# A one-core twelve-layer linear-attention kernel: the last bias's token shares move from the prologue to behind layer 2, and the first masking is left to VectorE

## The chip, the core and the metric

The kernel runs on one core of one Trainium2 chip. The metric is the device time of one execution in microseconds (us). The five engines are called by their short names: PE is TensorE (PEld is its weight load), DVE is VectorE, ACT is ScalarE, POOL is GpSimd, SP is SyncE, which here only issues transfers.

## The reference, cut to what matters

The input is x with 16 sequences of 256 tokens and 128 features. Twelve attention layers without a softmax follow each other, each with 16 heads of 8 features. After them come a layer norm, one gated feed-forward block with 384 hidden features, and a second layer norm.

```python
for i in range(12):
    qkv = x @ Wqkv[i].T + bqkv[i]
    q, k, v = split(qkv)                    # 16 heads of 8
    att = einsum('bhqd,bhkd->bhqk', q, k) / sqrt(8)
    y = einsum('bhqk,bhkd->bhqd', att, v)
    x = y @ Wproj[i].T + bproj[i] + x
x = layernorm(x0 + x)
x = layernorm(x + (silu(x @ wg.T) * (x @ wu.T)) @ wd.T)
```

Because nothing nonlinear stands between q, k and v, a layer acts on a sequence's tokens as one affine map. Everything about the tokens that a layer needs is their Gram matrix and their mean.

## The kernel before, in words

**What is tiled.** The 16 sequences form 8 pairs (`p`), and the pairs form two halves (`o`), four pairs each. For each sequence the kernel keeps a 128 x 128 matrix T and one more column, the token mean's image c; both lie in the tile `tst` (130 columns for a sequence, 260 for a pair). A layer updates T and c; the tokens themselves are only touched at the end, when T is applied to them and the feed-forward part runs.

**The prologue** (`prologue`) makes from each pair's tokens the Gram matrix (PE, L336), the means (DVE, L340 to L342), and the centred Gram matrix `g0` (tile `g`, DVE, L353, two instructions for a pair). L353 needs the mean laid out as a row, which PE transposes (L346) and ACT or DVE copies into `kv` (L205 or L207).

**One layer** has these steps. `products` multiplies T by the key and value weights (PE L434 to L436, from the second layer on), by the query weights (L442 to L444), and `g0` by the value side (L455; in the first layer straight from the raw weights `wraw`), and copies each result out of its accumulator bank. `heads` multiplies keys with that per group of 32 rows (L499), adds the offsets on DVE (L509, tile `gm`), keeps only the head blocks (the masking of `gm`, a multiplication by `mask32`, L213 by helper), and multiplies with the queries in 32 x 32 tiles (L517, "y" below). `projection` splits y into a high and a low part (`yhl`: the high part by ACT or DVE at L205 or L207, the low part by DVE at L530), multiplies by the projection weights (PE L534 to L536), adds to T on DVE (L541), and splits the new T (`thl`: high part on ACT at L205, low part on POOL at L210).

**Weights** are split the same way into `whl`: a copy by ACT or DVE (L205 or L207) and a subtraction by POOL (L210). SP then issues transfers that turn the projection weights (`wpt`, L305, L306). In the first layer's stage the weights of the layers 1 and 2 are split.

**The step that is moved.** `shares` has two DVE steps and one product: it adds the last layer's projection bias to the token means (L410), multiplies by the centring matrix on PE (L411, 128 x 16), and copies the result back to the tile `mb` (L412). Only the last layer reads `mb`.

**What sets the order.** Each engine runs its instructions strictly in the order in which the program holds them. That order is made when the kernel is built, by a list scheduler (`Plan.run`). Every step carries estimated costs for the engines that may do it, what it reads and writes, and a priority number, mostly the layer's number with small offsets. The scheduler repeatedly takes, among the steps that can start first, the one with the lowest priority number (with a tiny weight for the length of what depends on it), puts it on the engine where it is estimated to end first, and gives it one of eight accumulator banks. So a step that is given another place or other engines also moves other steps, and copies between ACT and DVE, elsewhere.

The first masking was free to go to either engine, and `shares` stood after the prologue with a priority near layer 8, although the scheduler takes a later priority early where nothing else can start:

```python
plan.op({DVE: dve(OB * 32), POOL: pool(OB * 32)}, lambda e: mul(e, gm, gm, mask32...), [], [vgm[o]], prio)
...
shares(L - 4)
```

Of the kernel before, what the change touches and what calls it, by code (L numbers as in the profile page):

```python
# [14 lines left out]
ALU = mybir.AluOpType  # L15
# [3 lines left out]
L = 12  # L19
# [19 lines left out]
OB = G * PB  # L39
# [34 lines left out]
PE, ACT, DVE, POOL, SP = "pe", "act", "dve", "pool", "sp"  # L74
# [100 lines left out]
def act(n, sbuf=False, pointers=0):  # L175
    return (94 if sbuf else 51) + 93 * pointers + n / 1.2


def dve(n, fast=False):
    return 69 + n / (1.92 if fast else 0.96)  # L180


def pool(n):
    return 147 + 2.1 * n
# [7 lines left out]
def linear_attention_ffn_kernel(ctx: ExitStack, tc: tile.TileContext, x, xt, wall, wq0, bias, wg, wu, wd, out):  # L192
    nc = tc.nc
# [5 lines left out]
    plan = Plan({"bank": 8, "raw": RAW, "weights": WSLOTS, "turned": WSLOTS})  # L199
# [12 lines left out]
    def mul(e, dst, a, b):  # L212
        (nc.vector if e == DVE else nc.gpsimd).tensor_tensor(dst, a, b, ALU.mult)  # L213
# [26 lines left out]
    bcol, wq0s = new("bcol", [L, 4]), new("wq0s", [C])  # L240
# [12 lines left out]
    mask32 = new("mask32", [32])  # L253
# [7 lines left out]
    vbias, vwq0 = Val(), Val()  # L261
# [53 lines left out]
    means = new("means", [B])  # L315
# [6 lines left out]
    vt, vc, vhi, vlo, vm, vg0, vkv, vyh, vyl, vqo, vw = (named() for _ in range(11))  # L322
# [34 lines left out]
    def center_tokens(p, prio):  # L357

        bs = slice(p * PB, (p + 1) * PB)
        x3 = xts[p].rearrange("p (b t) -> p b t", t=T)  # L360
        vn = Val()
        plan.op({POOL: 150}, lambda e: nc.gpsimd.tensor_scalar(nmeans[:, bs], means[:, bs], -1.0, 0.0, ALU.mult, ALU.add), [vm[p]], [vn], prio)
        for b in range(PB):
            plan.op({ACT: act(T, True, 1)}, lambda e, b=b: nc.scalar.activation(
                x3[:, b, :], x3[:, b, :], AF.Identity, bias=nmeans[:, p * PB + b : p * PB + b + 1]), [vn], [vx[p]], prio)
# [5 lines left out]
    def offset_products(l, o):  # L371

        raw, pc = wts[l][0], Val("bank")
        c = tst[:, o * OB : (o + 1) * OB, C]

        def mm():
            for s in range(1 if l else 0, 3):
                for g in range(G):
                    cols = slice(32 * g, 32 * g + 32)
                    nc.tensor.matmul(bank(pc)[cols, s * OB : (s + 1) * OB], wraw[raw.slot][:, s * C : (s + 1) * C][:, cols], c, start=True, stop=True)  # L380
        return [raw, *vc[o * G : (o + 1) * G]], pc, mm

    def offsets(l, o, prio, pc):


        bs, ps = slice(o * OB, (o + 1) * OB), slice(o * G, (o + 1) * G)
        c = tst[:, bs, C]
        step = lambda costs, f, reads, writes: plan.op(costs, f, reads, writes, prio)
        src = lambda s: bank(pc)[:, s * OB : (s + 1) * OB]
        step({DVE: 133}, lambda e: nc.vector.tensor_scalar(vb[:, bs], src(2), bcol[:, l, 2:3], None, ALU.add), [pc, vbias], [vvc[o]])  # L390
        step({DVE: 133}, lambda e: nc.vector.tensor_scalar(kb[:, bs], src(1), bcol[:, l, 1:2], float(T), ALU.add, ALU.mult), [pc, vbias], [vkb[o]])
        if l == 0:
            step({DVE: 133}, lambda e: nc.vector.tensor_scalar(qc[:, bs], src(0), bcol[:, 0, 0:1], None, ALU.add), [pc, vbias], [vqc[o]])
        step({DVE: dve(32 * OB)}, lambda e: nc.vector.transpose(flat(vbb[:, bs]), vb[:, bs].unsqueeze(2).to_broadcast([128, OB, 32])), [vvc[o]], [vvb[o]])
        step({DVE: dve(32 * OB)}, lambda e: mul(e, kvo[:, bs], vbb[:, bs], kb[:, bs].unsqueeze(2).to_broadcast([128, OB, 32])), [vvb[o], vkb[o]], [vkvo[o]])

        if l < L - 1:
            def share(e):
                if e == ACT:
                    nc.scalar.activation(c, c, AF.Identity, bias=bcol[:, l, 3:4])  # L400
                else:
                    nc.gpsimd.tensor_scalar(c, c, bcol[:, l, 3:4], 0.0, ALU.add, ALU.add)
            step({POOL: 200, ACT: 220}, share, [vbias, *(vhi[ps] if l else [])], vc[ps])

    mb, vmb = new("mb", [B]), Val()

    def shares(prio):

        pc = Val("bank")
        plan.op({DVE: 133}, lambda e: nc.vector.tensor_scalar(mb, means, bcol[:, L - 1, 3:4], None, ALU.add), [vbias, *vm], [vmb], prio)  # L410
        plan.op({PE: 214}, lambda e: nc.tensor.matmul(bank(pc)[:, :B], center, mb, start=True, stop=True), [vmb], [pc], prio)  # L411
        plan.op({DVE: 133}, lambda e: nc.vector.tensor_copy(mb, bank(pc)[:, :B]), [pc], [vmb], prio)  # L412

# [2 lines left out]
    vgm = sets()  # L416
# [55 lines left out]
    def first_offsets(o, prio):  # L472
        def fill(e):
            for p in range(o * G, (o + 1) * G):
                nc.gpsimd.tensor_copy(qss[p][:, :, C], qc[:, p * PB : (p + 1) * PB])
        plan.op({POOL: 600}, fill, [vqc[o]], vqo[o * G : (o + 1) * G], prio)

    def heads(l, o, prio, riders):

        raw = wts[l][0]
        pairs = range(o * G, (o + 1) * G)
        gm = gms[o]
        pm, pys = Val("bank"), [Val("bank") for _ in pairs]
        group = lambda g: slice(32 * (g % G), 32 * (g % G) + 32)
        src = [raw] if l == 0 else [vkv[p] for p in pairs]

        more = [(*r, *offset_products(*r)) for r in riders]

        def mm_m(e):
            for _, _, _, _, mm in more:
                mm()
            for p in pairs:
                for b in range(PB):
                    n = (p - o * G) * PB + b
                    tk = wraw[raw.slot][:, C : 2 * C] if l == 0 else kvs[p][:, b, 0, :]
                    for g in range(G):
                        nc.tensor.matmul(bank(pm)[group(g), n * 32 : n * 32 + 32], tk[:, group(g)], gvs[p][:, b, group(g)], start=True, stop=True)  # L499
        reads = [v for _, _, rs, _, _ in more for v in rs]  # L500
        if l == 0 and o == 1:

            reads += vw[:G]
        plan.op({PE: 890 + 140 * len(more)}, mm_m, [*(vgv[p] for p in pairs), *src, *reads], [pm, *(m[3] for m in more)], prio)
        for lo, oo, _, pc, _ in more:
            offsets(lo, oo, prio + (OFFSET if lo else 0), pc)
            if lo == 0:
                first_offsets(o, prio)
        plan.op({DVE: dve(OB * 32)}, lambda e: nc.vector.tensor_tensor(  # L509
            gm, bank(pm)[:, : OB * 32].rearrange("p (b j) -> p b j", j=32), kvo[:, o * OB : (o + 1) * OB], ALU.add), [pm, vkvo[o]], [vgm[o]], prio)  # L510
        plan.op({DVE: dve(OB * 32), POOL: pool(OB * 32)}, lambda e: mul(e, gm, gm, mask32.unsqueeze(1).to_broadcast([128, OB, 32])), [], [vgm[o]], prio)

        def mm_y(e):
            for b in range(PB):
                for r, p in enumerate(pairs):
                    for g in range(G):
                        nc.tensor.matmul(bank(pys[r])[group(g + r), b * W : (b + 1) * W], gm[group(g), r * PB + b, :], qss[p][group(g), b, :], start=True, stop=True)  # L517
        plan.op({PE: 1200}, mm_y, [vgm[o], *(vq[p] for p in pairs), *(vqo[p] for p in pairs)], pys, prio)
        return pys
# [68 lines left out]
    def prep_ffn(prio):  # L588
        for n, src in (("g", wg), ("u", wu), ("d", wd)):
            raw = Val("raw")  # L590
            ints = lambda raw=raw: wraw[raw.slot][:, : NH * C].bitcast(I32)
            plan.op({SP: 192 * 5}, lambda e, src=src, ints=ints: nc.sync.dma_start(ints(), src), [], [raw], prio)
            plan.op({ACT: act(384, True), DVE: dve(384, True)}, lambda e, n=n, ints=ints: copy(e, fw[n], ints()), [raw], [vfw[n]], prio)
# [152 lines left out]
    prep_weights(0)  # L746
    for p in range(NP):
        prologue(p, -1 if p < G else LATE)
    shares(L - 4)
    for o in range(NO):  # L750
        first_q(o, -0.5 if o == 0 else 0.03)
    for l in range(L):
        if l + 1 < L:
            prep_weights(l + 1)
        for o in range(NO):
            at = l + OSTEP * o
            for p in range(o * G, (o + 1) * G):
                products(l, p, at)
            for r, py in enumerate(heads(l, o, at, [(l, o)] * (l < OWN) + [(l + o, 1 - o)] * (OWN <= l + o < L))):
                projection(l, o * G + r, py, at + (LSTEP * r if l == L - 1 else 0))  # L760
        if l < NP:
            center_tokens(l, l + 2)
    prep_ffn(L - 2)
    picks(L - 4)
    for p in range(NP):
# [35 lines left out]
```

## Time and profile before

| what | value |
| --- | --- |
| three runs, median (lowest to highest) | 305.5 us (305.44 to 306.06) |
| the profiled execution's own time | 305.16 us |
| its span, first to last instruction | 303.2 us |
| around the span | 1.96 us |
| busy: PE, PEld, DVE, ACT, POOL | 294.3, 269.8, 226.1, 217.7, 137.8 us |
| granted PE clock over the span | 0.998 |

The profiled execution is 0.34 us shorter than the median of the three runs. A timeline row gives the start, the time from the first start to the last end of the group, the engine, the line, the operation, what is written and read, and how many instructions the row merges. On PE a 32-bit product shows as two instructions for each weight load in the program, so "x4" of L455 is one pair's two products.

### The profile page before, as it was taken

The numbers are of one execution on the slowest core, as the hardware profiler recorded it, in microseconds if no ns is written. First come the engines' busy times: TensorE is split into PE (matmuls) and PEld (weight loads), VectorE is DVE, ScalarE is ACT, GpSimd is POOL, SyncE is SP. The second block draws the span as 40 slices with busy tenths as digits, with TensorE's granted clock in tenths as the row PEclk, the third lists the DMA queues.
The fourth block names the chain that finished last, engine by engine and source line by source line (L and its number), as shares of the span: only waits on it lengthen the run. The fifth ranks groups of instructions, "written<-read, shape, count | busy, mean of one in ns | idle before, by whom it ended". The sixth has DMA issues, their size and how long they took to land.

```text
span 303.2 us, 12834 instructions
## 1 busy us (share of the span) xinstructions
PE 294.3 (97%) x5376; PEld 269.8 (89%) x5376; DVE 226.1 (75%) x683; ACT 217.7 (72%) x559; POOL 137.8 (45%) x208
## 2 busy tenths in 40 slices
PE   8999999999999999999999999999999999999981
PEld 8989999999999999999999999989999998878760
DVE  4796887777677676876767777786644789999993
ACT  3556877867777768777686666777887558788875
POOL 8256452334531445225432354224431167777883
PEclk9999999999999999999999999999999999999999
DMA  7624213112031120311302102120000000000225
GB/s 214 163 91 131 67 39 89 38 46 82 3 89 37 39 89 4 88 40 28 98 2 56 37 17 50 49 68 17 2 2 4 3 1 2 0 0 8 63 70 138
DMA packets 22489, 15.65 MB, mean 52 GB/s; under 512 B 1952, under 2 KB 19872, under 8 KB 22432
## 3 DMA queue, kind: packets, MB, share of 16 engines
q1 hardware_dynamic: 21872, 14.62, 17.3%
q8 instruction: 42, 0.69, 0.9%
q10 hardware_dynamic: 560, 0.22, 0.3%
q14 instruction: 15, 0.12, 0.1%
HBM read 8.02 MB, written 2.10 MB: 33 GB/s over the span
## 4 chain that ended last, share of the span: by engine, by line
PE 87%; DVE 10%; issue 1%; ACT 1%; POOLq 0%; POOL 0%; DVEq 0%
PE bank L455 14%; PE bank L434 8%; PE bank L517 8%; PE bank L436 7%; PE bank L435 7%; PE bank L442 5%; PE bank L499 5%; PE bank L536 4%; PE bank L534 4%; PE bank L535 4%; PE bank L443 3%; PE bank L444 3%; PE bank L336 3%; DVE st L618 2%; PE bank L706 2%; PE bank L707 2%
## 5 line engine op out<-in xcount | busy, mean ns | idle before, releaser
L210 POOL TENSOR_TENSOR thl<-tst,thl 128x260 fp32r<-128x260 f32 x88 | 64.8, 768 | 123.1 <-ACT thl L205 123.1
L205 ACT COPY qgv<-bank 128x256 f32<-128x256 f32 x169 | 59.8, 378 | 19.2 <-PE bank L444 12.9
L205 ACT COPY kv<-bank 128x512 f32<-128x512 f32 (+1 forms) x93 | 53.4, 575 | 19.5 <-PE bank L436 14.2
L434 PE MATMUL bank<-whl,thl 128*128 128x256 f32 x176 | 51.9, 295 | 0.0
L436 PE MATMUL bank<-whl,thl 128*128 128x256 f32 x176 | 49.7, 282 | 0.0
L435 PE MATMUL bank<-whl,thl 128*128 128x256 f32 x176 | 49.4, 281 | 0.0
L455 PE MATMUL bank<-kv,g 128*128 128x128 f32 x352 | 46.1, 275 | 0.0
L541 DVE TENSOR_TENSOR tst<-bank,tst 128x260 f32<-128x260 f32 x96 | 36.9, 425 | 9.4 <-PE bank L536 9.0
L205 ACT CAST thl<-tst 128x260 fp32r<-128x260 f32 x88 | 33.0, 408 | 14.6 <-DVE tst L541 14.5
L455 PEld LDWEIGHTS bank<-kv,g 128*128 128x128 f32 x352 | 42.7, 191 | 0.4 <-issue 0.4
L448 DVE TENSOR_SCALAR qgv<-bank,bcol 128x2 f32<-128x2 f32 x88 | 19.2, 221 | 28.3 <-ACT qgv L205 22.9
L434 PEld LDWEIGHTS bank<-whl,thl 128*128 128x128 f32 x176 | 33.1, 188 | 4.0 <-issue 3.8
L530 DVE TENSOR_TENSOR yhl<-bank,yhl 128x260 fp32r<-128x260 f32 x96 | 34.4, 420 | 2.2 <-ACT yhl L205 2.1
L436 PEld LDWEIGHTS bank<-whl,thl 128*128 128x128 f32 x176 | 33.1, 188 | 0.3 <-POOL thl L210 0.2
L435 PEld LDWEIGHTS bank<-whl,thl 128*128 128x128 f32 x176 | 33.2, 189 | 0.0
L442 PE MATMUL bank<-thl,whl 128*128 128x260 f32 x88 | 28.8, 327 | 0.0
L205 ACT CAST yhl<-bank 128x260 fp32r<-128x260 f32 (+1 forms) x61 | 21.8, 408 | 8.3 <-PE bank L517 7.7
L207 DVE CAST yhl<-bank 128x260 fp32r<-128x260 f32 (+1 forms) x43 | 16.7, 430 | 12.7 <-PE bank L517 12.7
L517 PE MATMUL bank<-qgv,gm 32*32 32x130 f32 x1536 | 25.8, 280 | 0.2 <-DVE gm L213 0.2
L443 PE MATMUL bank<-thl,whl 128*128 128x260 f32 x88 | 24.8, 282 | 0.0
L444 PE MATMUL bank<-thl,whl 128*128 128x260 f32 x88 | 24.7, 281 | 0.0
L517 PEld LDWEIGHTS bank<-qgv,gm 32*32 32x32 f32 x1536 | 17.2, 103 | 5.5 <-ACT kv L205 0.3
(157 smaller groups left out, 694.7 us busy)
## 6 DMA issues: line engine op xcount, KB each, us to landing
wraw<-wall SPq DMA_DIRECT2D x12, 256.0 KB, 3.0
wpt<-whl SPq DMA_DIRECT2D x24, 96.0 KB, 2.2
qgv<-x SPq DMA_DIRECT2D x8, 256.0 KB, 5.0
xt<-xt SPq DMA_DIRECT2D x8, 256.0 KB, 3.1
out<-kv SPq DMA_DIRECT2D x7, 256.0 KB, 2.3
wpt<-whl SPq DMA_DIRECT2D x24, 64.0 KB, 2.7
wpt<-whl SPq DMA_DIRECT2D x24, 32.0 KB, 1.9
wraw<-wg SPq DMA_DIRECT2D x1, 192.0 KB, 3.2
```

The costliest lines, as they stand in the source:

```text
L205: nc.scalar.copy(dst, src)
L210: (nc.vector if e == DVE else nc.gpsimd).tensor_tensor(dst, a, b, ALU.subtract)
L434: nc.tensor.matmul(o, hi[:, b, 0:C], hl(0, 1, 2), start=True, stop=False)
L435: nc.tensor.matmul(o, hi[:, b, 0:C], hl(1, 1, 2), start=False, stop=False)
L436: nc.tensor.matmul(o, lo[:, b, 0:C], hl(0, 1, 2), start=False, stop=True)
L442: nc.tensor.matmul(o, hl(0, 0), flat(hi), start=True, stop=False)
L443: nc.tensor.matmul(o, hl(0, 0), flat(lo), start=False, stop=False)
L444: nc.tensor.matmul(o, hl(1, 0), flat(hi), start=False, stop=True)
L455: nc.tensor.matmul(bank(pgv)[:, b * C : (b + 1) * C], g0[p][:, b, :], tv(b), start=True, stop=True)
L517: nc.tensor.matmul(bank(pys[r])[group(g + r), b * W : (b + 1) * W], gm[group(g), r * PB + b, :], qss[p][group(g), b, :], start=True, stop= ...
L530: plan.op({DVE: dve(PB * W)}, lambda e: nc.vector.tensor_tensor(yl, bank(py)[:, : PB * W], yh.bitcast(F32), ALU.subtract), [py, vyh[p]], [ ...
L541: plan.op({DVE: dve(PB * W)}, lambda e: nc.vector.tensor_tensor(ts, bank(pw)[:, : PB * W], ts, ALU.add), [pw], [vt[p], vc[p]], prio)
```

## The change

Two edits. `shares` is called within the loop over layers, after layer 2, with a priority of 4, and its first DVE step now also waits for the T of all pairs (`vt`). The masking of the first half in the first layer may only be done by DVE; every other masking can still go to either engine.

```diff
-    def shares(prio):
+    def shares(prio, behind):
 
         pc = Val("bank")
-        plan.op({DVE: 133}, lambda e: nc.vector.tensor_scalar(mb, means, bcol[:, L - 1, 3:4], None, ALU.add), [vbias, *vm], [vmb], prio)
+        plan.op({DVE: 133}, lambda e: nc.vector.tensor_scalar(mb, means, bcol[:, L - 1, 3:4], None, ALU.add), [vbias, *vm, *behind], [vmb], prio)
         plan.op({PE: 214}, lambda e: nc.tensor.matmul(bank(pc)[:, :B], center, mb, start=True, stop=True), [vmb], [pc], prio)
         plan.op({DVE: 133}, lambda e: nc.vector.tensor_copy(mb, bank(pc)[:, :B]), [pc], [vmb], prio)
...
-        plan.op({DVE: dve(OB * 32), POOL: pool(OB * 32)}, lambda e: mul(e, gm, gm, mask32.unsqueeze(1).to_broadcast([128, OB, 32])), [], [vgm[o]], prio)
+        masking = {DVE: dve(OB * 32)} if l + o == 0 else {DVE: dve(OB * 32), POOL: pool(OB * 32)}
+        plan.op(masking, lambda e: mul(e, gm, gm, mask32.unsqueeze(1).to_broadcast([128, OB, 32])), [], [vgm[o]], prio)
...
     for p in range(NP):
         prologue(p, -1 if p < G else LATE)
-    shares(L - 4)
...
         if l < NP:
             center_tokens(l, l + 2)
+        if l == 2:
+            shares(l + 2, vt)
```

In the built program this gives the following order. All transfers stand in the same order on SP.

- PE: L411 leaves its place between the fifth and sixth pair's L455 of the first layer and stands in layer 8, between the last L436 and the first projection product (L534). There, one pair's L455, which stood in that place, moves behind the projection. In the first layer the eighth pair's L455 moves from behind y to ahead of y.
- DVE: L410 stands after the last T sum of layer 2, L412 between the T sums of layer 8. The first masking stands behind the four L353 of the seventh and eighth pair.
- The split of layer 1's weights (`whl`, the high part) goes from DVE to ACT, ahead of two copies of `qgv`. One addition of a bias to c (L402, POOL) goes to ACT (L400).
- In the layers 1, 2 and 8 a few copies change between ACT and DVE (four copies of `qgv`, one of `kv`, and two pairs of `yhl` copies).

## The prediction

> **What bounds the kernel now.** I read the page's busy table and its chain first. PE is busy for 97% of the span, and the chain that ended last runs through PE for 87% of it.
>
> ```profile
> PE 294.3 (97%) x5376; PEld 269.8 (89%) x5376; DVE 226.1 (75%) x683; ACT 217.7 (72%) x559; POOL 137.8 (45%) x208
> PE 87%; DVE 10%; issue 1%; ACT 1%; POOLq 0%; POOL 0%; DVEq 0%
> ```
>
> Then the busy time by stages. The columns are the window, its length, and PE's, PEld's, DVE's, ACT's and POOL's busy time.
>
> ```profile
> 20.00:26.00 6.00, 5.78 (x123) 5.11 (x122) 4.86 (x16) 3.70 (x9) 3.96 (x9) 1.00 0.28 68
> 26.00:240.00 214.00, 213.84 (x4630) 200.26 (x4629) 152.27 (x471) 157.12 (x414) 80.10 (x112) 1.00 0.16 45
> ```
>
> From 26 to 240 us PE is idle for 0.16 us in all. There, work added to PE lengthens the run by its whole length, work added to DVE or ACT costs nothing while it stays under their slack, and a delay that arrives at 26 us goes through to the end. So two places decide: the first layer's stage, and the spot in layer 8 that takes L411.
>
> Next the timeline of the first layer's stage.
>
> ```profile
> 16.80 0.23 DVE L410 TENSOR_SCALAR mb<-means,bcol 128x16 f32<-128x16 f32 x1
> 16.94 0.42 DVE L509 TENSOR_TENSOR gm<-bank,kvo 128x256 f32<-128x256 f32 x1
> 17.19 0.38 ACT L205 COPY kv<-bank 128x256 f32<-128x256 f32 x1
> 17.27 1.11 DVE L353 SCALAR_TENSOR_TENSOR g<-kv,tmeans,bank 128x128 f32<-128x128 f32 x4
> 17.28 0.30 PEld L411 LDWEIGHTS bank<-mb,center 128*128 128x128 f32 x2
> 17.44 0.72 POOL L213 TENSOR_TENSOR gm<-gm,mask 128x256 f32<-128x256 f32 x1 [0.60 <-DVE gm L509]
> 17.59 0.37 ACT L205 COPY qgv<-bank 128x256 f32<-128x256 f32 x1
> 17.66 0.56 PEld L455 LDWEIGHTS bank<-wraw,g 128*128 128x128 f32 x4
> 18.30 0.42 DVE L207 CAST whl<-wraw 128x512 fp32r<-128x512 f32 x1
> 18.64 0.17 DVE L412 COPY mb<-bank 128x16 f32<-128x16 f32 x1
> 18.72 0.42 DVE L207 CAST whl<-wraw 128x512 fp32r<-128x512 f32 x1
> 18.80 1.47 POOL L210 TENSOR_TENSOR whl<-wraw,whl 128x512 fp32r<-128x512 f32 x1 [0.64 <-DVE mb L412]
> ```
>
> POOL masks beside DVE's four L353 and ends at 18.16. PE waits for L353: the first of the four ends at 17.61, and the seventh pair's L455 loads from 17.66. Its last load starts at 18.03 (17.66 + 0.56 - 0.19), and y starts 0.31 later. L411 at 17.28 fills a time in which PE would wait for L353 anyway. The weight loads of the next microseconds show y's start and two waits behind it:
>
> ```profile
> 18.34 0.80 PEld L517 LDWEIGHTS bank<-qgv,gm 32*32 32x32 f32 x64
> 20.50 0.19 PEld L536 LDWEIGHTS bank<-yhl,whl 128*128 128x128 f32 x1 [0.41 <-DVE yhl L530]
> 25.68 0.19 PEld L436 LDWEIGHTS bank<-whl,thl 128*128 128x128 f32 x1 [0.22 <-POOL thl L210]
> ```
>
> L536 waits for DVE's low part of y. DVE is dense from its first yhl cast at 19.35 to the last T sum at 22.80, so it hands a late y on unshortened, to ACT's and POOL's splits and to the wait at 25.68.
>
> **The change, part by part.**
>
> The masking. It leaves POOL, where it took 0.72 us, and costs 0.42 us on DVE (the other maskings there have a median of 0.416). The instruction is shorter, but it now queues behind the four L353. Without L410, L509 can start 0.14 earlier (16.94 - 16.80), at 16.80; the offsets it adds are ready at 16.75. The first L353 follows by 0.33, at 17.13, and the others by 0.26 each (1.11 = 0.34 + 3 x 0.26): the last starts at 17.91 and ends at 18.25. The third reads ACT's kv copy, which ends at 17.57, before its 17.65. The masking starts at 18.17 and ends at 18.59. Near 200 us, where y does wait for a masking on DVE, its first product starts 0.15 after the masking's end (200.47 to 200.61). That gives y at 18.74. PE's own route gives the same: the eighth pair's L455, now ahead of y, loads its second product 0.05 after 18.25, at 18.30, its last pass 0.11 later at 18.41, and y follows 0.31 after that, at 18.72. So y starts at 18.74 instead of 18.34: **+0.40**. The product moved ahead of y (four loads at 0.11) brings nothing back: after y, PE waits for casts. y's first cast on ACT came 0.91 after y's start (19.25), now at 19.65; DVE's casts come at 19.75, the low part at 20.43, and L536 at 20.90. The bounds: if L509 doesn't gain its 0.14, both routes are as much later, and the term is +0.54; if y's delay is eaten by the waits at 20.50 (0.48 over the usual spacing of 0.12) and 25.68 (0.29 over it), it is 0 (below nothing: the gain among the rivals). I keep 0.40, since it is made of rows of this very place.
>
> [...]
>
> The weights' split. Layer 1's high part (0.42 on DVE) goes to ACT. No row shows this form there; the nearest, the 128x512 cast of hh on ACT, takes 0.64. ACT's copy at 17.59 lets it start at 17.93, so it ends at 18.57, and POOL's low part starts 0.08 later, at 18.65, instead of 18.80. It ends before the 20.27 of now and nothing on the path waits for it. ACT's two qgv copies end by 19.2, before the cast at 19.65. Cost 0, as long as DVE's other split, now at 18.51 (0.34 behind the masking), comes first; see the second rival.
>
> L410 and L412 as DVE work (0.14 and 0.17). L410 lands behind layer 2's sums, ahead of 0.69 us in which DVE waits for ACT; L412 between layer 8's sums, whose following chain has the wmean steps (0.7 us) put behind it in exchange. Cost 0; if the slack were gone, 0.3.
>
> L411 in layer 8. These rows show its new place:
>
> ```profile
> 173.55 0.28 PE L436 MATMUL bank<-whl,thl 128*128 128x256 f32 x1
> 173.67 0.61 PE L455 MATMUL bank<-kv,g 128*128 128x128 f32 x4
> 174.03 0.37 PE L534 MATMUL bank<-yhl,whl 128*128 128x260 f32 x1
> ```
>
> PE has no gap here. L411's two loads are 0.11 apart in the prologue, so it adds 2 x 0.11 = **+0.22**. It was free before and is paid for now. It waits for no one (mb is ready since layer 2, and its bank's copy was done near 171 us). L412 needs it at about 175 and it is done at 174. The bounds are 0.22 and 0.31 (one further wait of PE costs about 0.09, as where L436 is followed by L517).
>
> Copies that change engines in layers 1, 2 and 8, and the bias on ACT (0.31). In layer 1 the masking ends at 35.22 and y's first load follows at 35.26, with no slack. DVE loses a copy (0.41), but it now waits for ACT's fourth qgv copy before L509; ACT has 0.4 more to do there. By the rows L509 comes 0 to 0.10 later: **+0.05**. In layers 2 and 8 the maskings have 0.3 us and more of slack: 0.
>
> Sum: 0.40 + 0.22 + 0.05 = 0.67. The profiled execution, 303.2 of span and 1.96 around it, goes from 305.16 to 305.83. The median of the runs lies 0.34 higher, so I forecast 305.5 + 0.67 = 306.2 us. About 0.2%, or 0.61 us, is what a measurement of this kernel can tell from no change, so this forecast stands just beyond the bound.
>
> **The rivals.**
>
> Absorbed: the late y is eaten by waits that PE had anyway (0.48 at 20.50, 0.29 at 25.68). Then only L411 is left: +0.22, 305.7, not told from no change. For it speaks that PE idles there; against it, that these waits are for DVE and POOL, which both start from y. It decides if L536's wait shrinks by what y is late.
>
> The port. DVE and POOL block each other on copies between SBUF tiles:
>
> ```profile
> 198.04 1.29 POOL L210 TENSOR_TENSOR whl<-wraw,whl 128x512 fp32r<-128x512 f32 x1
> 198.22 1.32 DVE L207 CAST wfu<-wraw 128x384 fp32r<-128x384 int32 x1
> ```
>
> The cast started after POOL and ended 0.21 after POOL's end. In the changed stage, DVE's split starts at 18.51 and POOL's at 18.65. If POOL comes first by as little as 0.14, DVE is held until 18.6 + 1.29 + 0.21 = 20.1, and its yhl cast comes at 20.05 instead of 19.75: 0.30 more, in all +0.97, 306.5. [...]
>
> A gain: the stage's waits vanish. POOL's four T splits there take 0.86 each against 0.77 over the run. Should POOL, without the masking, and DVE, without a split and two mb steps, come out of each other's way, all of PE's idle time there (0.48, 0.29 and 0.12 at 24.70) could go: 0.89 less, with L411's 0.22 paid, -0.67, 304.8. Against it: DVE sat idle for 0.21 before its cast at 19.35, so it wasn't its earlier work that was late. It decides if y starts no later than 18.34.
>
> **How the numbers follow.** My sum holds with 0.54, spread from about +0.4 to +0.85, so that seven parts in ten of it are slower by over the bound; absorbed 0.17; port 0.14; gain 0.15, most of it beyond the bound. Slower: 0.38 + 0.14 = 0.52. Faster: 0.12. The rest, 0.36, is within. The range reaches from a partial gain (305.2) to the port with its bounds (306.7), and leaves out the full gain and some stray.
>
> **What would show it.** Right: y's first load near 18.74, L537 (the former L536) waiting until about 20.9, everything near 26 us 0.4 later, L411's two loads near 174 with PE solid around them. Wrong: y at 18.4 or L537's wait shortened (absorbed or gain), DVE's whl cast over 1 us (port), a PE gap in layer 1 or 8, or a feed-forward stage of another length than now.

## The result and the profile after

The changed kernel takes 306.23 us (median of 14 runs, 305.37 to 306.97). The kernel before, run beside it on the same chip, takes 305.56 us (14 runs, 304.55 to 306.54). The ratio is 1.0028, with a 95% interval of 1.0015 to 1.0041: slower by 0.67 us between the medians and 0.74 between the means. The profiled execution took 306.18 us, with a span of 304.3.

The page's busy table and the engine line of its chain:

```profile
PE 295.1 (97%) x5376; PEld 270.7 (89%) x5376; DVE 226.7 (75%) x681; ACT 219.1 (72%) x563; POOL 137.0 (45%) x206
PE 87%; DVE 10%; issue 1%; ACT 1%; POOLq 0%; POOL 0%; DVEq 0%
```

PE still sets the time. The stages (window, its length, busy time of PE, PEld, DVE, ACT and POOL):

```profile
20.00:26.00 6.00, 5.47 (x138) 4.78 (x119) 5.50 (x17) 3.37 (x9) 3.36 (x5) 1.00 0.22 52
26.00:240.00 214.00, 213.84 (x4586) 200.32 (x4600) 152.23 (x471) 158.29 (x417) 80.12 (x111) 1.00 0.17 46
```

From 26 to 240 us PE is idle for 0.16 us, as before. In the first layer's stage it is idle for 0.53 us (6.00 - 5.47), where it was 0.22.

The timeline of the first layer's stage, and of the spot in layer 8. Lines above 510 have moved by one: y is L518, the projection L535 to L537, the low part of y L531.

```profile
17.21 0.42 DVE L509 TENSOR_TENSOR gm<-bank,kvo 128x256 f32<-128x256 f32 x1
17.54 1.11 DVE L353 SCALAR_TENSOR_TENSOR g<-kv,tmeans,bank 128x128 f32<-128x128 f32 x4
17.93 1.07 PEld L455 LDWEIGHTS bank<-wraw,g 128*128 128x128 f32 x8 [0.17 <-DVE g L353]
18.26 0.62 ACT L205 CAST whl<-wraw 128x512 fp32r<-128x512 f32 x1
18.57 0.42 DVE L213 TENSOR_TENSOR gm<-gm,mask 128x256 f32<-128x256 f32 x1
18.91 0.42 DVE L207 CAST whl<-wraw 128x512 fp32r<-128x512 f32 x1
18.97 1.49 POOL L210 TENSOR_TENSOR whl<-wraw,whl 128x512 fp32r<-128x512 f32 x1 [1.72 <-ACT whl L205]
19.13 0.85 PEld L518 LDWEIGHTS bank<-qgv,gm 32*32 32x32 f32 x64
20.13 0.77 DVE L207 CAST yhl<-bank 128x260 fp32r<-128x260 f32 x2 [0.81 <-PE bank L518]
21.28 0.19 PEld L537 LDWEIGHTS bank<-yhl,whl 128*128 128x128 f32 x1 [0.52 <-DVE yhl L531]
26.46 0.19 PEld L436 LDWEIGHTS bank<-whl,thl 128*128 128x128 f32 x1 [0.20 <-POOL thl L210]
...
174.39 0.19 PEld L436 LDWEIGHTS bank<-whl,thl 128*128 128x128 f32 x1
174.51 0.31 PEld L411 LDWEIGHTS bank<-mb,center 128*128 128x128 f32 x2
174.74 0.19 PEld L535 LDWEIGHTS bank<-yhl,whl 128*128 128x128 f32 x1
```

Everything here is later than foreseen: y starts at 19.13 and not at 18.74. But as much, 0.40 us, arose at the very start, where the program had not been changed. The first and the last weight loads of L336, before's rows first and after's in the second fence:

```profile
4.35 2.12 PEld L336 LDWEIGHTS bank<-qgv 128*128 128x128 f32 x16 [0.20 <-issue]
15.06 0.97 PEld L336 LDWEIGHTS bank<-qgv 128*128 128x128 f32 x8
```

```profile
4.24 2.64 PEld L336 LDWEIGHTS bank<-qgv 128*128 128x128 f32 x16
15.46 0.97 PEld L336 LDWEIGHTS bank<-qgv 128*128 128x128 f32 x8
```

The same first 16 loads take 2.12 us in one execution and 2.64 in the other. In both they start about 0.2 us apart and then drop to 0.11. The drop comes at 4.92 us in before and at 5.89 us in after, where the trace's record of the granted clock starts its full-speed stretch. So two executions must not be compared by the clock on the wall. Below I measure each moment from the last load of L336, which starts at 15.84 us in before (15.06 + 0.97 - 0.19) and at 16.24 in after.

| us behind the last load of L336 | before | after | difference |
| --- | --- | --- | --- |
| y's first load | 2.51 | 2.89 | +0.38 |
| the projection's load that waits for the low part | 4.66 | 5.04 | +0.38 |
| first load of L434 (layer 1) | 7.11 | 7.47 | +0.36 |
| ninth load of L434 (layer 1, second half) | 17.19 | 17.73 | +0.54 |
| a load of L434 in layer 7 (ahead of L411) | 127.10 | 127.65 | +0.55 |
| first load of L434 behind L411 | 163.43 | 164.18 | +0.74 |
| last load of L434 (layer 11) | 213.38 | 214.12 | +0.74 |
| end of the span | 287.36 | 288.10 | +0.74 |

The difference comes in three steps, and it stays to the end: at y, within layer 1, and at L411's place.

### The profile page after: what moved, and what is told of

Read it like the earlier page. It is cut to its first block, busy times and chain, and to the rows that moved or that the text cites. A ratio compares the mean times of both kernels' runs of the same rounds, so it can differ in the third digit from the quotient of the medians.

```text
span 304.3 us, 12839 instructions
## 1 busy us (share of the span) xinstructions
PE 295.1 (97%) x5376; PEld 270.7 (89%) x5376; DVE 226.7 (75%) x681; ACT 219.1 (72%) x563; POOL 137.0 (45%) x206
## 4 chain that ended last, share of the span: by engine, by line
PE 87%; DVE 10%; issue 1%; ACT 1%; POOLq 0%; POOL 0%; DVEq 0%
PE bank L455 14%; PE bank L434 8%; PE bank L518 8%; PE bank L436 7%; PE bank L435 7%; PE bank L442 5%; PE bank L499 5%; PE bank L537 4%; PE bank L535 4%; PE bank L536 4%; PE bank L443 3%; PE bank L444 3%; PE bank L336 3%; DVE st L619 2%; PE bank L707 2%; PE bank L380 2%
## 5 line engine op out<-in xcount | busy, mean ns | idle before, releaser
L205 ACT COPY qgv<-bank 128x256 f32<-128x256 f32 x172 | 60.8, 378 | 17.9 <-PE bank L444 12.6
L434 PE MATMUL bank<-whl,thl 128*128 128x256 f32 x176 | 51.9, 295 | 0.0
L436 PE MATMUL bank<-whl,thl 128*128 128x256 f32 x176 | 49.7, 282 | 0.0
L455 PE MATMUL bank<-kv,g 128*128 128x128 f32 x352 | 45.9, 275 | 0.0
L455 PEld LDWEIGHTS bank<-kv,g 128*128 128x128 f32 x352 | 42.6, 191 | 0.4 <-issue 0.4
L434 PEld LDWEIGHTS bank<-whl,thl 128*128 128x128 f32 x176 | 33.1, 188 | 4.0 <-issue 3.8
L531 DVE TENSOR_TENSOR yhl<-bank,yhl 128x260 fp32r<-128x260 f32 x96 | 34.3, 417 | 2.2 <-ACT yhl L205 2.1
L436 PEld LDWEIGHTS bank<-whl,thl 128*128 128x128 f32 x176 | 33.1, 188 | 0.3 <-POOL thl L210 0.2
L518 PE MATMUL bank<-qgv,gm 32*32 32x130 f32 x1536 | 25.8, 280 | 0.2 <-DVE gm L213 0.2
L518 PEld LDWEIGHTS bank<-qgv,gm 32*32 32x32 f32 x1536 | 17.3, 103 | 5.4 <-ACT kv L205 0.3
```

The source lines that it names most:

```text
L205: nc.scalar.copy(dst, src)
L434: nc.tensor.matmul(o, hi[:, b, 0:C], hl(0, 1, 2), start=True, stop=False)
L436: nc.tensor.matmul(o, lo[:, b, 0:C], hl(0, 1, 2), start=False, stop=True)
L455: nc.tensor.matmul(bank(pgv)[:, b * C : (b + 1) * C], g0[p][:, b, :], tv(b), start=True, stop=True)
L531: plan.op({DVE: dve(PB * W)}, lambda e: nc.vector.tensor_tensor(yl, bank(py)[:, : PB * W], yh.bitcast(F32), ALU.subtract), [py, vyh[p]], [ ...
```

## The experiments

**Theory.** The change costs 0.38 us because the masking queues on DVE behind four L353, and 0.2 us because L411 is paid on a full PE. **Rivals.** The port: DVE's split of layer 2's weights is held by POOL's step. Absorbed: the delay of y is eaten by waits that PE has anyway. Chance: part of the 0.67 us is how the executions fell.

**The changed kernel again, each edit alone, and L411 nine times.** The first is the changed kernel as it is, with one comment line more. The edits of the others:

```diff
# mask_only: the kernel before, with
+        masking = {DVE: dve(OB * 32)} if l + o == 0 else {DVE: dve(OB * 32), POOL: pool(OB * 32)}
+        plan.op(masking, ...)
# shares_only: the kernel before, with
-    shares(L - 4)
+        if l == 2:
+            shares(l + 2, vt)
# l411_nine: the changed kernel, with
-        plan.op({PE: 214}, lambda e: nc.tensor.matmul(bank(pc)[:, :B], center, mb, start=True, stop=True), ...)
+        plan.op({PE: 214}, lambda e: [nc.tensor.matmul(bank(pc)[:, :B], center, mb, start=True, stop=True) for _ in range(9)], ...)
```

> The changed kernel unaltered, profiled a second time. In the first profiles the changed kernel's PE went over from weight loads 0.21 us apart to loads 0.11 us apart at 5.9 us, the kernel before at 5.0 us, and this alone put the changed one 0.41 us back before the changed code begins. Theory A: that moment is chance and differs between executions of one program; then it comes at another time here in some profiles, y's first load is again 13.2 us (19.13 - 5.91) behind it, where it was 12.8 us (18.34 - 5.50) in the kernel before, and the time is 0.6 to 0.9 us over the kernel before. Rival: the change itself moves it; then it stays at 5.9 here and at 5.0 in every kernel with the old prologue. A second question: the pause of 0.13 us inside the L499 loads near 32 us (layer 1), which the kernel before did not have. If it belongs to the order of instructions it is here again, at the same load; if it is chance it is gone or elsewhere.

> The first masking on DVE, the shares left in the prologue. Theory: the masking queues behind the four L353, and L410 keeps its 0.14 us ahead of L509, so y starts 0.54 us later than in the kernel before (0.40 + 0.14), L411 costs nothing, and the time is 0.5 us over the kernel before. Port rival: here L412 stands between the masking and DVE's split of layer 2's weights, so that split starts at about 18.72 in the kernel before's time, behind POOL's at 18.65; then DVE's cast takes over 1 us, its yhl cast is held to about 20.05 and the time is 0.7 us over. Absorbed rival: 0 to 0.1 over.

> The shares behind layer 2, the first masking free again for DVE or POOL (it stands on POOL). Theory: without L410, L509, the four L353 and POOL's masking come 0.14 us earlier and y with them (-0.14); L411 in layer 8 costs two loads, +0.22. Sum +0.08, not told from the kernel before; PE's step of +0.2 stands near 174 us in the trace. Rival, L411 free in layer 8 as in the prologue: -0.14, and no step near 174 us. Rival, the cost of the change sits in the shares: +0.6.

> The changed kernel with L411 nine times at its place in layer 8 (the eight others write the same result again). Theory: PE has no gap there, each further product costs its two loads of 0.11 us, so 8 x 0.22 = 1.8 us over the changed kernel and about 2.5 us (0.8%) over the kernel before. Rival, the place has slack or the waits of the projection behind it absorb it: under 0.5 us over the changed kernel.

Before ran beside these four with a median of 305.54 us (23 runs).

| kernel | median, us (runs) | ratio to before, 95% | y behind the last L336 load | load that waits for the low part |
| --- | --- | --- | --- | --- |
| again_after | 306.43 (5) | 1.0030 [1.0018, 1.0042] | 2.89 | 5.34 |
| mask_only | 305.99 (12) | 1.0017 [1.0006, 1.0028] | 3.02 | 5.36 |
| shares_only | 305.53 (12) | 1.0000 [0.9988, 1.0012] | 2.37 | 5.63 |
| l411_nine | 308.16 (6) | 1.0076 [1.0057, 1.0095] | 2.88 | 5.04 |

L411 is settled. Nine products in place of one cost 308.16 - 306.43 = 1.73 us against the repeat beside it on the same chip (1.93 against the 306.23 of the result), where 8 x 0.22 = 1.76 was expected. The trace has the loads in one row (l411_nine, timeline):

```profile
175.15 2.09 PEld L411 LDWEIGHTS bank<-mb,center 128*128 128x128 f32 x18
```

That is (2.09 - 0.31) / 8 = 0.22 us for each further product, to the hundredth what the prologue's spacing gave.

y's terms are settled too: 2.89 again in the repeat, +0.51 with the masking alone, -0.14 with the shares alone, and 0.51 - 0.14 = 0.37.

What releases y last is a closer matter. The prediction gave two routes, the masking's end (18.74) and PE's own way through the eighth pair's L455, which now stands ahead of y (18.72). The trace has PE's own route last, by a hair. In the changed kernel y's first load stands 0.31 us behind PE's last load of L455 (18.82 to 19.13), as in before (18.03 to 18.34) and in all eleven profiles in which L455 stands right ahead of this y. That spacing is PE's own: near 46 us of before it is 0.31 too, though the masking had ended 0.70 us earlier. The masking ends at 18.99, 0.14 ahead of y, where 0.12 is enough in the three kernels below that have no L455 right ahead of y. So the two routes end within about 0.02 us of each other. Both run through DVE's queue, since the eighth pair's L455 waits for the last L353, and both come with the masking edit. The 0.38 us is shown for the edit; no run here parts the masking from the moved product. (In the trace of before, L411 stands between the sixth and seventh pair's L455, with 24 of their loads ahead of it, and not between the fifth and sixth.)

The start is chance, as the repeat's expectation had it, though the repeat alone doesn't show it: full speed comes at 5.86 us there and at 5.89 in after. But it comes at 4.33 in shares_only and at 5.08 and 6.62 in two more kernels with the moved shares, and at 4.63 and 6.39 in two executions of one kernel that keeps the old prologue (before_split_late and before_late_again below).

But the row behind y, the load that waits for the low part, was later than the theory in three of the four. Here is why. In mask_only the port rival came true:

```profile
18.85 1.29 POOL L210 TENSOR_TENSOR whl<-wraw,whl 128x512 fp32r<-128x512 f32 x1 [1.72 <-ACT whl L205]
19.01 1.41 DVE L207 CAST whl<-wraw 128x512 fp32r<-128x512 f32 x1
20.34 0.75 DVE L207 CAST yhl<-bank 128x260 fp32r<-128x260 f32 x2
```

With L412 still ahead of it, DVE's split came 0.16 us behind POOL's step, took 1.41 us in place of 0.42, and ended at 20.42, 0.28 us behind POOL's end. In the changed kernel the same two stand 0.06 us apart the other way round (18.91 and 18.97); DVE needed 0.42, and POOL 1.49 in place of 1.29. On the clock mask_only is 0.45 us over before, nearer to the theory's 0.5 than to the port rival's 0.7; its profile shows one execution, a long one of its twelve (306.56), and not how often DVE is held so. The port is only my name for the rival: the two pairs of rows show that the step that starts second takes longer (1.41 us in place of 0.42, 1.49 in place of 1.29), not by what.

In shares_only and in the repeat a third thing held the same split, which I had not thought of (shares_only, then again_after, whose lines stand one further on):

```profile
19.59 0.43 DVE L207 CAST whl<-wraw 128x512 fp32r<-128x512 f32 x1 [1.39 <-DMA wraw<-wall]
21.08 0.19 PEld L536 LDWEIGHTS bank<-yhl,whl 128*128 128x128 f32 x1 [1.51 <-DVE yhl L530]
```

```profile
19.69 0.78 DVE L208 CAST whl<-wraw 128x512 fp32r<-128x512 f32 x1 [0.75 <-DMA wraw<-wall]
21.54 0.19 PEld L538 LDWEIGHTS bank<-yhl,whl 128*128 128x128 f32 x1 [0.82 <-DVE yhl L532]
```

The split of layer 2's weights, which no step of the first layer reads, stands in DVE's queue ahead of the casts of y, and waits for its 256 KB. (The repeat's cast then met POOL's step, which ran until 20.19, and took 0.78.) The 256 KB landed at 17.73 us in before and 17.93 in after, but at 19.57 in shares_only and 19.67 in the repeat, 3.1 to 5.2 us after the issue. All these kernels have this trap. Whether it springs is chance: after and its repeat hold the same program, and it sprang in one of the two.

**The pair without the trap.** So I took the split out of the way in both kernels and compared them again. In these two it also reads the first layer's high-part T, and so stands behind it on DVE.

```diff
-        plan.op({ACT: act(n, True), DVE: dve(n, True)}, lambda e: copy(e, whl[hl.slot][:, 0, a:], wraw[raw.slot][:, a:]), [raw], [hl], prio)
+        plan.op({ACT: act(n, True), DVE: dve(n, True)}, lambda e: copy(e, whl[hl.slot][:, 0, a:], wraw[raw.slot][:, a:]), [raw, *([vhi[0]] if l == 2 else [])], [hl], prio)
```

> The kernel before with one value more that the high-part split of the third layer's weights (L207 whl, 128x512) reads: the first layer's high-part T, so that the split stands in DVE's queue behind the first layer's splits and no longer ahead of them. Nothing is left out of the computation. Theory (the split, when its 256 KB transfer lands late or POOL is in a step, holds DVE's casts of yhl and through them L536 and L537): y's first load stays 2.5 us behind the last load of L336, the high-part wait stays 4.5 to 4.7 us behind it in every execution, where it was 4.66 to 5.63 in profiles of kernels with the split ahead; the median is 0 to 0.3 us below that of the kernel before (305.2 to 305.6). Rival (the late transfer is beside the path in most executions): within 0.1 us of the kernel before. Rival against: the split, put behind, is late for the third layer's own loads or holds the second layer's casts, 0.3 to 0.8 us slower.

> The changed kernel with the same one value more at the split of the third layer's weights. Nothing is left out. To be read against before_split_late, where neither kernel can wait for that transfer at the first layer's casts. Theory (masking 0.36 to 0.40 us at y, L411's load and product 0.20 to 0.22 in the stage that PE fills): y's first load 2.9 us behind the last load of L336, 0.56 to 0.62 us longer than before_split_late, and 0.3 to 0.6 over the kernel before. Rival (part of the changed kernel's 0.28 us over before is the split held by POOL or by its transfer, not the masking): 0.2 to 0.35 us longer than before_split_late.

(The 0.28 us of the second expectation's rival is the 0.28% of the ratio; between the medians it was 0.67 us.) Before had a median of 305.70 us beside these (35 runs). before_split_late took 304.99 (12 runs, ratio 0.9986 [0.9975, 0.9997]), after_split_late 306.00 (12 runs, 1.0015 [1.0001, 1.0029]). The first lies 0.2 us below what I expected, the second at the low end of it, and their difference, 1.01 us, above the 0.56 to 0.62. The timelines of PE, before_split_late first, show that the mechanism holds all the same:

```profile
18.24 0.80 PEld L517 LDWEIGHTS bank<-qgv,gm 32*32 32x32 f32 x64
20.40 0.19 PEld L536 LDWEIGHTS bank<-yhl,whl 128*128 128x128 f32 x1 [0.41 <-DVE yhl L530]
...
161.26 0.80 PEld L517 LDWEIGHTS bank<-qgv,gm 32*32 32x32 f32 x64
```

```profile
18.69 0.85 PEld L518 LDWEIGHTS bank<-qgv,gm 32*32 32x32 f32 x64
20.85 0.19 PEld L537 LDWEIGHTS bank<-yhl,whl 128*128 128x128 f32 x1 [0.52 <-DVE yhl L531]
...
161.85 1.00 PEld L518 LDWEIGHTS bank<-qgv,gm 32*32 32x32 f32 x64
```

Behind the last load of L336 y comes at 2.51 and 2.88, the waiting load at 4.67 and 5.04, layer 1 at 7.06 and 7.42: +0.37, +0.37 and +0.36. At the ninth L434 it is +0.29, so layer 1 costs nothing here. L411 adds 0.21 at its place. Of the other 0.5 us of this pair's 1.01, two thirds are pauses. The same 64 small loads of y took 1.00 us in place of 0.80 (the last rows of the two fences), and those of an earlier layer (55.27 us) 0.96. What is left of the 0.5 us creeps in at 0.01 to 0.02 us a layer; I know no cause for it. In the slower y of the last row PE paused for 0.20 us ahead of the 59th load, while the profile shows nothing that it waited for. In mask_only the same y had the longest such pause, ahead of its 56th load:

```profile
162.32 0.72 PEld L518 LDWEIGHTS bank<-qgv,gm 32*32 32x32 f32 x55
163.53 0.15 PEld L518 LDWEIGHTS bank<-qgv,gm 32*32 32x32 f32 x9 [0.49 <-issue]
```

The page lists a queue of the kind "instruction" (queue, packets, MB, share; from before):

```profile
q8 instruction: 42, 0.69, 0.9%
```

Its packets are 16 KB each. I took from the trace when the packet ahead of this y ended, counted from y's first load, and how long it was from the first to the last of the 64 loads:

```
packet's end    -1.22 -0.89 -0.87 -0.81 -0.80 -0.72 -0.70 -0.66 -0.61 -0.48 -0.44 -0.43 -0.21 -0.14
first to last    0.70  0.70  0.70  0.70  0.70  0.70  0.70  0.70  0.72  0.85  0.96  0.89  1.17  1.26
```

All 14 profiles of this study are in it. At this y a packet that ended 0.66 us ahead or earlier cost nothing (0.70 us from first to last); with a later one PE stood still, and went on 1.27 to 1.36 us after the packet's end. The pauses at 56 us (in after_split_late and two kernels below) ended 1.41 to 1.43 behind theirs. A late packet alone is not enough: in before one ended 0.20 us ahead of the y at 64.02 us, in after one 0.06 us ahead of that at 142.89, and both took 0.70. The trace doesn't say which engine a packet is for. That PE waits for its instructions in these pauses is my reading of the order; no run moved a packet to test it.

**A better place for the masking.** If the wait for DVE's queue is what costs, the add and the masking as one step of DVE, ahead of the four L353, should gain.

```diff
-        plan.op({DVE: dve(OB * 32)}, lambda e: nc.vector.tensor_tensor(gm, ..., ALU.add), [pm, vkvo[o]], [vgm[o]], prio)
-        plan.op({DVE: dve(OB * 32), POOL: pool(OB * 32)}, lambda e: mul(e, gm, gm, mask32...), [], [vgm[o]], prio)
+        if l + o == 0:
+            plan.op({DVE: 2 * dve(OB * 32)}, lambda e: (add(e), keep(e)), [pm, vkvo[o]], [vgm[o]], prio - 1)
+        else:
...
-    shares(L - 4)
+        if l == 0:
+            shares(L - 4, [vgm[0]])
```

> The kernel before, with the first layer's add of kvo and its masking made one step of the list for DVE, ahead of the four L353, and with the last bias's shares made behind that masking in the first layer (not in the prologue, not in a middle layer). Nothing is left out. Theory (y is released by DVE's queue: with the two steps of 0.42 us ahead of the four L353 in place of behind them, and no POOL step of 0.87 between): y's first load about 0.6 us earlier behind the last load of L336 (1.8 to 2.0 in place of 2.51); of that 0.3 to 0.4 us stays where PE has loads to run, the rest turns into the wait for the sums behind it: 0.4 to 0.8 us faster than the kernel before. Rival (the four L353 then end later, and their pairs' products with them: PE waits there for what it no longer waits for at y): within 0.2 us. Rival against: the third layer's split takes DVE just ahead of the casts of yhl, as in mask_only: 0.2 to 0.6 us slower.

> mask_fused_shares with the split of the third layer's weights behind the first layer's high-part T as in before_split_late. Nothing is left out. Theory: y's first load 1.8 to 2.0 us behind the last load of L336, high-part wait no later than 4.3 behind it, 0.5 to 1.0 us faster than the kernel before. Rival: as mask_fused_shares, PE waits elsewhere, within 0.2 us of before_split_late.

mask_fused_shares took 305.36 us (12 runs, ratio 0.9987 [0.9974, 1.0000]), fused_split_late 306.25 (12 runs, 1.0017 [1.0005, 1.0029]). The first gained less than expected, with an interval that reaches to no gain; the second lost. In both y starts at 2.03, where 1.8 to 2.0 was expected: so the order on DVE does set y. But the load that waits for the low part comes at 5.08, later than before's 4.66. Of mask_fused_shares:

```profile
18.92 1.27 POOL L210 TENSOR_TENSOR whl<-wraw,whl 128x512 fp32r<-128x512 f32 x1 [1.72 <-ACT whl L205]
19.19 1.03 DVE L410 TENSOR_SCALAR mb<-means,bcol 128x16 f32<-128x16 f32 x1
20.14 0.75 DVE L207 CAST yhl<-bank 128x260 fp32r<-128x260 f32 x2
```

L410, an addition of 16 columns that took 0.23 us in the prologue, started 0.27 us behind POOL's step, took 1.03 and ended 0.03 behind POOL's end, and the casts of y queued behind it: the hold of mask_only again, by another instruction. What fused_split_late loses on the other is only partly seen. In its profile full speed begins at 6.71 us and not at 5.87, and its last transfer lands 2.48 us after its issue, where it is 1.95 in before and in after. The first is worth 0.49 us at the last load of L336, the second 0.52, and the two profiled executions differ by 0.91. But the medians of twelve runs differ by 0.89 as well, and why these two should come more often in this kernel is open.

**The last four: the base again, and each edit alone without the trap.** mask_fused_late is fused_split_late with the shares left in the prologue; the other three are before_split_late, alone and with the edit of mask_only or shares_only.

> before_split_late once more, on the chip of the next three, to be their base. Nothing is left out. Theory (it takes a wait of DVE for a transfer and for POOL out of the first layer): 0.3 to 0.8 us faster than the kernel before; high-part and low-part products 4.65 us behind the last load of L336 as in before_split_late. Rival (its 305.0 was a lucky set of moments of the clock): within 0.2 us of the kernel before.

> before_split_late with the change's masking edit alone: the first half's masking of the first layer on DVE, the shares left in the prologue. Nothing is left out. Theory (masking queues behind L410, L509 and four L353): y's first load 0.51 us later than in before_split_late (3.0 behind the last load of L336), L537 as much later (5.15 to 5.2), and 0.5 us on the median. Rival (the delay of y is absorbed by waits PE has anyway): 0 to 0.2 us. Rival (POOL's step still takes DVE, as in mask_only: L412 or a cast held for over 0.5): L537 5.4 or later.

> before_split_late with the change's shares edit alone: L410, L411 and L412 behind layer 2's T, the masking left to POOL. Nothing is left out. Theory: y's first load 0.14 earlier than in before_split_late (2.37), L536 4.5 to 4.55 behind the last load of L336, and 0.20 to 0.22 paid in layer 8: 0 to 0.1 us slower than before_split_late. Rival (the shares cost nothing in layer 8, or their gain at L509 is not handed on): -0.15 or +0.25.

> before_split_late with the add and the masking of the first half as one step of DVE ahead of the four L353, the shares left in the prologue, so that L410 is not behind the masking, where POOL's step held it for 1.03 us. Nothing is left out. Theory (DVE's casts of yhl no longer wait for POOL): y's first load 2.15 to 2.2 behind the last load of L336, the low-part product 4.3 to 4.5 in place of 4.67, 0.15 to 0.35 us faster than before_split_late. Rival (ACT, which has the second layer's split ahead of its yhl cast, and the copies of qgv set the end of y): low part at 4.6 to 4.7, within 0.1 us of before_split_late. Rival against (something of fused_split_late beside L410's hold made it 0.9 us slower than mask_fused_shares): 0.4 to 0.9 us slower than before_split_late.

Before had a median of 305.65 us beside these (35 runs).

| kernel | median, us (runs) | ratio to before, 95% | y | waiting load | first L434 |
| --- | --- | --- | --- | --- | --- |
| before_late_again | 305.57 (12) | 0.9996 [0.9984, 1.0009] | 2.51 | 4.67 | 7.06 |
| mask_only_late | 306.20 (12) | 1.0020 [1.0009, 1.0031] | 3.02 | 5.23 | 7.64 |
| shares_only_late | 305.26 (12) | 0.9993 [0.9982, 1.0004] | 2.37 | 4.53 | 6.91 |
| mask_fused_late | 305.83 (11) | 1.0007 [0.9992, 1.0023] | 2.57 | 5.02 | 7.43 |

The same kernel has now given medians of 304.99 and 305.57, so a median of 12 runs is worth about 0.3 us here, and some 0.3 of the 1.01 us of the pair above was that. Over its 24 runs the mean is 305.28, and before's 70 runs beside them have a mean of 305.64: taking the split out of the way gains about 0.36 us. It is the best version that I have, by 0.1%, with an uncertainty of 0.2 us either way. In the second set alone it could not be told from before, as its rival had it. Against that base (24 runs, two chips) the three others have means of +0.90 (mask_only_late), +0.07 (shares_only_late) and +0.74 us (after_split_late, 306.02), each uncertain by some 0.3.

The moments in the trace are as expected for both single edits, with no part lost to the trap: the masking costs 0.51 at y and 0.58 at layer 1, the shares give 0.14 to 0.15 and take 0.21 to 0.23 at L411 (0.18 ahead of before_late_again until layer 8, and 0.02 behind it at the last L434). So for the waiting load and the rows up to L411 the absorbed rival is out in every pair. The median of shares_only_late lies 0.31 us below before_late_again's, where 0 to 0.1 above was expected; medians of 12 runs don't settle so little. The profile of mask_only_late ends 1.16 us behind its base's, on the same count; the 0.58 beyond layer 1 stands in a pause of 0.31 us like those above (56.49 us), and behind the landing of the last output, where both kernels with the masking alone end 0.29 us later than the others; I know no cause for that.

mask_fused_late misses: it was to be 0.15 to 0.35 us faster than its base and is 0.3 to 0.5 slower. Its timeline:

```profile
18.13 0.43 DVE L213 TENSOR_TENSOR gm<-gm,mask 128x256 f32<-128x256 f32 x1 [0.51 <-DVE gm L509]
18.68 1.12 PEld L522 LDWEIGHTS bank<-qgv,gm 32*32 32x32 f32 x64 [0.82 <-issue]
19.90 0.76 DVE L207 CAST yhl<-bank 128x260 fp32r<-128x260 f32 x2 [0.23 <-PE bank L522]
```

Put directly behind the add, the masking started after 0.51 us in which DVE was idle, which the profile puts down to the add; in mask_fused_shares it was 0.10 (17.16 + 0.42 to 17.68), and why it is more here I don't know. So the place ahead of the four L353 brought the masking from 2.47 us behind the last load of L336 (mask_only_late) to 2.03, and y from 3.02 to 2.57, no earlier than the 2.51 of the base. The 64 loads of y then took 1.12 us in place of 0.80, and the four late L353 pushed two pairs' products behind y. In the profile the last transfer landed late here too, as in fused_split_late (2.67 us from issue, 1.94 in the base).

## Why the prediction was right

The direction and the size were right, 306.2 against 306.23 us. That the two agree to 0.03 us is luck, since a median of so few runs is worth about 0.3. The mechanism is judged by the moments in the trace, point by point in the order of its sum:

1. **PE is full from 26 us, so a delay that arrives goes through.** Right. Between before and after the differences at layer 1, layer 8 and the end only grow (0.36, 0.74, 0.74).
2. **The masking, +0.40.** Measured +0.38 at y and +0.36 at layer 1 against before, +0.37 and +0.36 in the pair without the trap. The bound of 0.54, for L509 without its 0.14, is the case of the masking alone: +0.51 there. Shares alone gave the 0.14 back. Of the two waits behind y the first did not shrink but grew (0.41 to 0.52 at the low part), so nothing was absorbed at the first, and 0.02 us at most up to layer 1. Both of the prediction's routes to y came out; PE's own was last by about 0.02 us.
3. **The split of layer 1's weights on ACT, 0.** Right, by little. Without the 0.40 us of the start, ACT ends at 18.48 (foreseen 18.57), DVE's split starts at 18.51 (18.51) and POOL's at 18.57 (18.65). The margin of the port rival was not 0.14 but 0.06 us, and mask_only, with L412 between, fell on the other side. The rival was a real one, and the changed kernel missed it narrowly. Its price was smaller than the 0.30 of the prediction: the waiting load stood at 5.36 in mask_only and at 5.23 with the same edit and no trap, 0.13 less.
4. **L410 and L412 on DVE, 0.** Nothing in the trace speaks against it: the lead of 0.12 us that shares_only_late has over before_late_again behind layer 1 does not shrink until layer 8. No run takes them apart from L411.
5. **L411 in layer 8, +0.22.** Measured 0.19 in the changed kernel (0.55 to 0.74), 0.21 in after_split_late, 0.23 in shares_only_late, and 0.22 for each of eight more.
6. **Layer 1's copies, +0.05.** Mis-sized in the profile after, where layer 1 costs 0.17. Of it 0.12 is a pause of PE within the 64 loads of L499 at 32.28 us. That pause isn't the change's. The repeat, whose layer 1 costs 0.32 in all behind the sprung trap, has one of 0.14 there, but l411_nine, whose first layers are the same, has none and is 0.02 us longer than before in layer 1; before_split_late has one of 0.09 and after_split_late none, and that pair gains 0.07. Without the pauses layer 1 costs 0.05 in the one pair and 0.02 in the other. The reason given for the term is not shown. The prediction has the second half's y at 35.26, right behind the masking's end at 35.22; in the trace of before its first load stands at 35.37, 0.32 behind PE's load before it, and in after the masking ends 0.32 ahead of that y. What ends these short pauses at L499 is open; they do not follow the instruction packets as those of the y near 161 us do.

The gain rival is out as well: y starts later in both pairs, and the three waits that were to vanish are all there (in after at 21.28, 25.48 and 26.46).

What the prediction left out is the scatter. The granted clock's full-speed stretch begins at a moment of its own in each execution (4.33 to 6.71 us), layer 2's weights land when they land (3.1 to 5.2 us after their issue), and PE pauses now and then (up to 0.56 us) while the profile shows nothing that it waits for. Each is worth as much as the terms of the sum. On the profile's own basis the forecast was 305.83 and the execution took 306.18, 0.35 more, and the start alone is worth 0.40. The medians average such things out in part.

## What to carry to other kernels

Read the moment of a step against a mark just ahead of the changed code, not against the start of the span: here 0.40 us of the visible delay had come earlier, by chance. A step that is early in a strict queue, and that nobody needs soon, was a trap here when it waited for a transfer (1.39 us in shares_only) or came behind POOL's step (1.41 us in place of 0.42 in mask_only): putting it behind the urgent work gained about 0.36 us (0.2 either way). And a step taken from an idle engine to a busy one is priced by its place in that queue, not by its duration: the masking ran 0.3 us faster on DVE (0.42 us, 0.72 on POOL) and, with the shares left where they were, y came 0.51 us later.

## What was not expected of the hardware

- The granted clock's full-speed stretch begins between 4.33 and 6.71 us in the 14 profiles, 1.2 us either way. For each microsecond that it comes later, the last load of L336 comes 0.46 us later, by a straight line through the 14 (15.45 at 4.33, 16.68 at 6.71). The stretch lasted 296.96 us in ten of them and 293.55 in the four others; no run shows what sets its start or its length.
- A product of 64 small loads (near 161 us, 0.70 us from first to last) took up to 0.56 us longer where a 16 KB packet of the instruction queue ended less than 0.66 us ahead of it; that the packet is the cause is my reading of the order in 14 profiles, and not shown.
- A 256 KB transfer issued at the same place landed 3.1 to 5.2 us later (at 17.73 us in before, at 19.57 in shares_only).
- VectorE's addition of 16 columns (L410) took 1.03 us beside a POOL step that had started 0.27 us earlier, where it takes 0.23 in the prologue of the kernel before.
